# A recommender with attention over 200 history rows: items gathered whole, shorter user steps, and part of the head's second layer on GpSimd

## The chip, the cores and the metric

The kernel runs on one core of a Trainium2 chip, in float32. The metric is the device time of one execution in microseconds. Several executions are timed and their median is given; one further execution is recorded by the hardware profiler, and all views of the profile (chain of waits, costliest groups, timeline, windows) are of that one. The engines are named as in the profile: PE is TensorE, PEld its weight loads, DVE is VectorE, ACT is ScalarE, POOL is GpSimd, SP is SyncE, which only issues DMAs. ACTq and SPq are DMAs issued on these engines' queues.

## The reference

There are 16384 samples, each with a user id, an item id, a category id and a history of 200 item ids. User and item tables have 100000 rows of 64 floats, the category table has 1000.

```python
u, it, c = u_emb[user], i_emb[item], c_emb[cate]
h = i_emb[hist]                                  # 200 x 16384 x 64
feat = concat([h, itb, h - itb, h * itb], -1)    # itb: it for every history row
a = dice(feat @ au_W1 + au_b1, au_alpha, axis=1) # 36 units, moments over the samples
w = a @ au_W2 + au_b2
cur = sum(w * h, axis=0)
z = concat([u, it, c, cur], -1)                  # 256 features
z = dice(z @ W1 + b1, alpha1, axis=0)            # 80 -> here 64 and 16 units
z = dice(z @ W2 + b2, alpha2, axis=0)
out = z @ W3 + b3

def dice(x, alpha, axis):
    p = sigmoid((x - mean(x, axis)) * rsqrt(var(x, axis) + 1e-8))
    return x * (p + alpha * (1 - p))
```

## The kernel before

The samples are cut into 8 column tiles of 2048 (`ND = 8`, index `c`). A column tile is `TD = 16` gathers of 128 rows: one gather is one indirect DMA on GpSimd (line 125), which writes 128 rows of 64 floats into one of 16 places of a buffer `rows`. There are five `rows` buffers. VectorE transposes a full buffer into a tile of features by samples (four instructions of line 153), 128 partitions by 1024 columns: two groups of 64 features, each with half of the samples. Line 158 is the helper `layer`, which does almost all matmuls, in halves of 512 columns.

**Side tiles.** For six of the eight column tiles, `SIDES = (1, 3, 4, 5, 6, 7)`, the sixteenth set of 128 rows is not gathered. Its rows are asked for one by one, with 256-byte DMAs whose addresses are read from `addrs`, some on SP's queue and some on ScalarE's (line 323, helper `ask`); column tile 5 does so in one history row of three. When all 128 have landed, VectorE passes a fence (line 344) and copies them into `rows` (line 387). GpSimd so issues fewer gathers.

**Prologue.** The items' rows are fetched and transposed to `itT[0..7]`, one column tile after the other (`fetch_all`, `ask_all`, then `place_tile` and `transpose`, lines 538 to 554). Between them the category embeddings are built by matmul: for each of 16 halves `q` VectorE makes eight one-hot tiles (line 501, ring of eight `xs`), TensorE multiplies them by the category table in two groups of 64 columns (line 505), ScalarE copies the sum out (line 509) and sends it to DRAM (line 516). `attention_weights` runs at the first column tile, `head_weights` (63 DMAs on SP and some VectorE work) after the last. Both order the engines' work by hand: under `tc.manual_schedule` each engine runs its instructions in the order written.

**History.** 200 history rows by 8 column tiles are 1600 steps `k`; 180 rows run in a hardware loop of two passes, 20 are written out. `step(k)` fetches rows for `k`, transposes and multiplies for `k - 1`, evacuates and measures `k - 2`, and weighs and adds into `curT` for `k - 9`, once the moments of that history row are known.

**User steps.** At the end ten steps `j` fetch the user rows, finish the last history steps, and do the first layer of the head for `c = j - 1`: `px` gets the 64 + 64 units of `w1a`, `ph[:32]` the other 16 + 16 of `w1b`. The products of category, item and `curT` come first, then those of the user rows (line 671). ScalarE evacuates `px` (line 623) and `ph` (line 631, 32 partitions by 512 columns, twice), VectorE takes batch statistics (line 581). In each step ScalarE also computes a gate (line 361) of a history step still to be weighed, VectorE the product `y` (line 364), and TensorE `wb` of both.

**Rest of the head.** After the moments (lines 590 to 613), the second layer runs over `c`: `dice` does a sigmoid on ScalarE (line 684), an affine on ScalarE (line 686) for odd `c` or else on VectorE (line 688), and a product on VectorE (line 689); then the matmuls of `w2a`, and those of `w2b` (line 705) for four column tiles at a time, in 32-row quarters. Then come moments again, the third layer, transposes, the bias and the output's DMAs.

Of the kernel before, what the change touches and what calls it, by code (L numbers as in the profile page):

```python
# [36 lines left out]
def din_kernel(  # L37
# [76 lines left out]
    ids = [make(f"ids{i}", P, NC, dt=I32) for i in range(2)]  # L114
    side = [make(f"side{i}", P, D) for i in range(3)]
# [117 lines left out]
    w2b = make("w2b", P, P)  # L233
    w3 = make("w3", P, 4, P)
    b1a = make("b1a", P, 1)
    b1b = make("b1b", S, 1)
# [9 lines left out]
    def head_weights():  # L246
        for t in (w1a, w1b, w2a, w2b, w3, bias2, al2):
            nc.vector.memset(t, 0.0)
        w1 = W1.rearrange("(f d) z -> d f z", d=D)
        for e in range(2):  # L250
            for g in range(2):
                r, d = quarter(e, g), ts(e, S)
                for f in (slice(0, 2), slice(3, 4)):
                    nc.sync.dma_start(w1a[r, f, ts(g, ZA)], w1[d, f, :ZA])
                    nc.sync.dma_start(w1b[r, f, ts(g, ZB)], w1[d, f, ZA:])
        for g in range(2):

            nc.sync.dma_start(w1a[ts(g, D), 2, ts(g, ZA)], w1[:, 2, :ZA])
            nc.sync.dma_start(w1b[ts(g, D), 2, ts(g, ZB)], w1[:, 2, ZA:])
            nc.sync.dma_start(w2a[ts(g, ZA), g * ZA : g * ZA + Z2], W2[:ZA])  # L260
            nc.sync.dma_start(b1a[ts(g, ZA)], col(b1)[:ZA])
            nc.sync.dma_start(ala[ts(g, ZA)], col(alpha1)[:ZA])
            nc.sync.dma_start(b1b[ts(g, ZB)], col(b1)[ZA:])
            nc.sync.dma_start(bias2[g * ZA : g * ZA + Z2], col(b2))
            nc.sync.dma_start(al2[g * ZA : g * ZA + Z2], col(alpha2))
            for j in range(4):
                r = slice(j * S + g * ZB, j * S + (g + 1) * ZB)
                nc.sync.dma_start(w2b[r, g * ZA : g * ZA + Z2], W2[ZA:])
                w = j * S + g * ZO
                nc.sync.dma_start(w3[g * ZA : g * ZA + Z2, j, w : w + ZO], W3)  # L270
                nc.sync.dma_start(alb[r], col(alpha1)[ZA:])
        nc.sync.dma_start(bias3, b3.partition_broadcast(P))
        for t, u in ((ala, al1a), (alb, al1b), (al2, al12)):
            nc.vector.tensor_scalar(u, t, -1.0, 1.0, ALU.mult, ALU.add)

        for t, n in ((same_a, ZA), (same_b, ZB)):
            nc.vector.tensor_single_scalar(lane, lanes, n - 1, ALU.bitwise_and)
            nc.vector.tensor_copy(t, lane)
            nc.vector.tensor_scalar(t, t, 0.0, n / P, ALU.is_equal, ALU.mult)
# [57 lines left out]
    def ask_all(s, split, first, n, at, table):  # L337
        for queue, runs in enumerate(shares(NS * P // ND, s, split)):
            runs = [(r0, min(end, n * P)) for r0, end in runs if r0 < n * P]
            ask(queue, runs, first, range(n), at, table)  # L340

# [47 lines left out]
    def fetch_all(k, c, ids, table):  # L389
        for n in range(TD - (c in SIDES)):  # L390
            j = column(c, n)
            gather(rows[k % ROWS], ids[:, j : j + 1], n, table)
# [91 lines left out]
    def order_categories():  # L484
        for c in range(ND):
            n, j = TD - (c in SIDES), column(c, 0)
            nc.scalar.dma_start(cs[c][:, :n], columns(r_cate)[:, j : j + n])
            if c in SIDES:
                j = column(c, TD - 1)
                nc.scalar.dma_start(cs[c][:, n:], col(r_cate[j * P : (j + 1) * P]))  # L490
        nc.scalar.dma_start(table, c_emb.rearrange("(b p) d -> p b d", p=PB))
# [26 lines left out]
    with tc.manual_schedule():  # L518
        nc.sync.dma_start(ids[0], columns(r_item))
        load_addresses(2, r_item.rearrange("(o b) -> o b", o=1))  # L520
        nc.vector.memset(hm, 0.0)
        nc.scalar.copy(hT[SPREAD], hm)
        order_categories()
        load_hist_ids(0, 0)
        load_addresses(0, r_hist[0:1])
        nc.sync.dma_start(ids[1], columns(r_user))
        nc.gpsimd.iota(lanes, pattern=[[1, P]], base=P, channel_multiplier=-1)
        for q in range(SPREAD - 1):
            spread_categories(q)
# [4 lines left out]
        scale_addresses(2)  # L534
# [3 lines left out]
        for c in range(ND + 1):  # L538
            if c < ND:
                fetch_all(c, c, ids[0], i_emb)  # L540
                ask_all(c, 0.56, -NS, NS, addr[2], i_emb)
                for q in (2 * c, 2 * c + 1):
                    pick_categories(q)
                    if q + SPREAD - 1 < HALVES:
                        spread_categories(q + SPREAD - 1)
                    if q:
                        store_categories(q - 1)
            if c == 0:
                attention_weights()
                scale_addresses(0)  # L550
            if c:
                if c - 1 in SIDES:
                    place_tile(c - 1, SIDES.index(c - 1) - NS)
                transpose(itT[c - 1], rows[(c - 1) % ROWS])
# [12 lines left out]
        head_weights()  # L567
# [10 lines left out]
    zst = [make(f"zst{i}", P, n, STATS) for i, n in enumerate((2 * ND, 4, 2 * ND))]  # L578

    def measure_head(i, j, t, h):  # L580
        nc.vector.bn_stats(zst[i][:, 2 * j + h, :], t[:, ts(h, CH)])

# [34 lines left out]
    def head_layer(pairs):  # L617
        layer(px, [(w1a[:, f], t) for f, t in pairs], last=False)
        layer(ph[:S], [(w1b[:, f], t) for f, t in pairs], last=False)
# [6 lines left out]
    def head_units(c):  # L626
        evacuate(za[c], px, b1a, 0, c)
        if c == ND - 1:
            start_moments("z", 0, 2, 0, same_a)
        for h in range(2):  # L630
            nc.scalar.activation(
                zb[c // 4][ts(c % 4, S), ts(h, CH)], ph[:S, ts(h, CH)], AF.Identity, bias=b1b
            )
            if c % 4 == 3:
                measure_head(1, c // 4, zb[c // 4], h)

    with tc.manual_schedule():
        steps(BODY, L - BODY, L - BODY, r_user.rearrange("(o b) -> o b", o=1))
        U = addr[(L - BODY) % 3]
        j = column(SIDES[-1], TD - 1)  # L640
        nc.sync.dma_start(sidx[0], col(r_user[j * P : (j + 1) * P]))
        first = -(-tiles_by_address(L - BODY)[0] // 3) * 3

        weighed = {*range(-LAG, K - LAG), K, K + 1}
        for j in range(ND + 2):
            if j < ND:
                fetch_all(K + j, j, ids[1], u_emb)
                if j == SIDES[-1]:
                    gather(rows[(K + j) % ROWS], sidx[0], TD - 1, u_emb)
                nc.sync.dma_start(category[j % 2], catT[j])  # L650
            step(K + j, K - 1, weighed)
            weighed.add(K + j - LAG)
            left = [k for k in range(K) if k not in weighed]
# [5 lines left out]
            if j < ND:  # L659
                ask_all(j, SPLIT, first, NS - 1, U, u_emb)  # L660
            if 1 <= j <= ND:
                c = j - 1
                head_layer(((2, category[c % 2]), (1, itT[c]), (3, curT[c])))
                if c in SIDES[:-1]:
                    place_tile(K + c, first + SIDES.index(c))
                parts = (0, TD) if c < ND - 1 else (0, TD - 4, TD)
                for n in map(slice, parts, parts[1:]):
                    transpose(user[c % 2], rows[(K + c) % ROWS], n)
                    for dst, w in ((px, w1a[:, 0]), (ph[:S], w1b[:, 0])):
                        for i in range(2):  # L670
                            nc.tensor.matmul(
                                by_tile(dst, i)[:, n], w, by_tile(user[c % 2], i)[:, n],
                                start=False, stop=n.stop == TD, skip_group_check=True,
                            )
                head_units(c)
# [4 lines left out]
        def dice(dst, z, norm, al1, al, parts=1, scalar=False):  # L680
            p = temps[next(turns) % len(temps)]
            for i in range(parts):
# [4 lines left out]
                else:  # L687
                    nc.vector.tensor_scalar(p[:, c], p[:, c], al1, al, ALU.mult, ALU.add)
                nc.vector.tensor_mul(dst[:, c], p[:, c], z[:, c])
# [5 lines left out]
        ab = ucT[:2]  # L695

        beside = {0: range(4), 4: range(4, 6), 6: range(6, 8)}
        for c in range(ND + 2):
            if c < ND:
                if c % 4 == 0:  # L700
                    dice(ab[c // 4], zb[c // 4], nb, al1b, alb, 2 if c == 0 else 1, c > 0)
                for i in range(2):
                    for k in beside.get(c, ()):
                        r = ts(k % 4, S)
                        nc.tensor.matmul(
                            pz[k % 4][:, ts(i, CH)], w2b[r], ab[k // 4][r, ts(i, CH)],
                            start=True, stop=False, skip_group_check=True,
                        )
                dice(curT[c], za[c], na, al1a, ala, 2 if c == 0 else 1, c % 2 == 1)
                layer(pz[c % 4], [(w2a, curT[c])], first=False)  # L710
# [70 lines left out]
```

## Time and profile before

| | |
|---|---|
| time, median of 3 runs | 31195.79 us (31191.82 to 31199.41) |
| profiled execution, its own time | 31199.79 us |
| its span in the profile | 31198.0 us |
| mean granted TensorE clock | 0.809 |
| PE, PEld busy | 20922.2 us (67%), 8551.5 us (27%) |
| DVE busy | 15705.3 us (50%) |
| ACT busy | 3823.8 us (12%) |
| POOL busy | 23418.8 us (75%), 24783 instructions |
| DMA | 907.51 MB, mean 29 GB/s |

Busy time does not count the issue of a DMA by its engine, so an engine that issues one DMA after the other shows as busy for only part of the time. In the groups, a line gives engine, operation, output and inputs, the count, busy time and mean duration, and at the end how long the engine had been idle just before these instructions, with what ended most of that. In the timeline a line gives start, duration, engine, line, operation, and in brackets the idle time before it and what released it; instructions of one kind that follow each other closely are put into one line with their count.

### The profile page before, as it was taken

The page shows a single profiled execution, that of the slowest core. Times are in us where ns is not written, and L with a number is a line of the kernel's source. Part 1 is how long each engine was busy: PE and PEld are TensorE (multiplying, and loading weights), DVE is VectorE, ACT ScalarE, POOL GpSimd, SP SyncE. Part 2 cuts the span into 40 slices and gives each one's busy share as a digit, 9 for nine tenths or more (in the row PEclk, how much of TensorE's full clock was granted, in tenths as well). Part 3 has the DMA queues.
Part 4 walks back from the last instruction along what each step waited for, and adds up shares of the span by engine and source line. Part 5 has one row for each costly group of instructions (what it writes and reads, how often), then busy time and mean ns, then how long its engine had stood idle before and what let it go on. Part 6 is the DMA issues. An engine that isn't in the chain of part 4 may idle for free.

```text
span 31198.0 us, 427397 instructions
## 1 busy us (share of the span) xinstructions
PE 20922.2 (67%) x39376; PEld 8551.5 (27%) x39376; DVE 15705.3 (50%) x21745; ACT 3823.8 (12%) x3330; POOL 23418.8 (75%) x24783
## 2 busy tenths in 40 slices
PE   5666666666666666666666666666666666666667
PEld 2222222222222222222222222222222222222222
DVE  4555554554555555555455455555555555545554
ACT  1111111111111111111111111111111111111111
POOL 6777777777777777777777777777777777777776
PEclk7888888888888888888888888887888888888888
DMA  2111111111111111111111111111111111111111
GB/s 41 29 29 29 29 29 29 29 29 29 29 29 29 29 29 29 29 29 29 29 29 29 29 29 29 29 29 29 29 29 29 29 29 29 29 29 29 29 29 30
DMA packets 1135469, 907.51 MB, mean 29 GB/s; under 512 B 730704, under 2 KB 730704, under 8 KB 1132426
## 3 DMA queue, kind: packets, MB, share of 16 engines
q0 software_dynamic: 792896, 813.51, 13.9%
q1 hardware_dynamic: 193404, 35.89, 0.8%
q10 hardware_dynamic: 146125, 30.64, 0.7%
q14 instruction: 2734, 22.39, 0.2%
q8 instruction: 310, 5.08, 0.1%
HBM read 873.55 MB, written 4.39 MB: 28 GB/s over the span
## 4 chain that ended last, share of the span: by engine, by line
POOL 32%; issue 12%; PE 5%; DMA 4%; DVE 2%; ACTq 1%; ACT 0%; DVEq 0%; POOLq 0%
POOL rows L125 32%; DMA rows<-in_L_rec_i_emb,idx 4%; PE px L158 2%; PE ph L158 1%; PE wb L158 1%; ACTq L323 1%; DVE hT L153 1%; DVE wb L368 0%; DVE curT L369 0%; ACT pg L361 0%; DVE st L377 0%; ACTq L315 0%; ACT xs L372 0%; DVE y L364 0%; DVE hm L400 0%
## 5 line engine op out<-in xcount | busy, mean ns | idle before, releaser
L125 POOL DMA_INDIRECT rows<-in_L_rec_i_emb,idx x24400 | 23038.6, 944 | 7542.4 <-issue 7198.7
L158 PE MATMUL ph<-hT,unit 128*128 128x512 f32 x6404 | 5928.7, 1077 | 9820.7 <-DVE hT L153 9820.2
L368 DVE SCALAR_TENSOR_TENSOR wb<-wb,au_bias,hT 128x1024 f32<-128x1024 f32 x1609 | 2080.3, 1293 | 9802.6 <-PE wb L158 9802.6
L158 PEld LDWEIGHTS ph<-hT,unit 128*128 128x128 f32 x6404 | 1747.3, 305 | 12865.9 <-DVE hT L153 12687.8
L153 DVE STREAM_TRANSPOSE hT<-rows 64x512 f32<-64x512 f32 x6404 | 4517.0, 705 | 1483.9 <-DMA rows<-in_L_rec_i_emb,idx 894.5
L158 PE MATMUL px<-hT,blk_h 128*128 128x512 f32 x6404 | 4125.0, 733 | 0.0
L372 ACT ACTIVATE xs<-px,au_bias 128x1024 f32<-128x1024 f32 x1602 | 1783.6, 1113 | 14375.2 <-PE wb L158 10720.9
L158 PE MATMUL wb<-y,blk_p 128*128 128x512 f32 x6436 | 3318.4, 597 | 246.6 <-DVE y L364 246.1
L361 ACT ACTIVATE pg<-xs,sh,rs 128x1024 f32<-128x1024 f32 x1609 | 1943.0, 1208 | 12481.6 <-issue 9985.6
L158 PE MATMUL px<-itT,blk_i 128*128 128x512 f32 x6404 | 3355.8, 606 | 0.0
L158 PE MATMUL wb<-xs,blk_x 128*128 128x512 f32 x6436 | 3300.5, 594 | 5.3 <-DVE curT L369 5.3
L158 PE MATMUL px<-hm,blk_m 128*128 128x512 f32 x6408 | 3011.2, 592 | 0.0
L400 DVE TENSOR_TENSOR hm<-ph,itT 128x1024 f32<-128x1024 f32 x1601 | 1960.6, 1225 | 1920.1 <-PE ph L158 1920.0
L364 DVE TENSOR_TENSOR y<-pg,xs 128x1024 f32<-128x1024 f32 x1609 | 1959.4, 1218 | 1293.7 <-ACT pg L361 1291.5
L158 PEld LDWEIGHTS px<-hT,blk_h 128*128 128x128 f32 x6404 | 1649.9, 258 | 2417.9 <-issue 2363.7
L377 DVE BATCH_NORM_STATS2 st<-xs 128x6 f32<-128x512 f32 x3204 | 2058.9, 685 | 60.8 <-ACT xs L372 17.1
L369 DVE TENSOR_TENSOR curT<-wb,curT 128x1024 f32<-128x1024 f32 x1609 | 1970.4, 1225 | 54.8
L158 PEld LDWEIGHTS px<-itT,blk_i 128*128 128x128 f32 x6404 | 1402.0, 219 | 2031.2 <-issue 2031.2
L158 PEld LDWEIGHTS wb<-y,blk_p 128*128 128x128 f32 x6436 | 1215.2, 191 | 1847.9 <-issue 1460.7
L158 PEld LDWEIGHTS wb<-xs,blk_x 128*128 128x128 f32 x6436 | 1224.6, 190 | 1551.9 <-issue 1544.4
L158 PEld LDWEIGHTS px<-hm,blk_m 128*128 128x128 f32 x6408 | 1217.4, 190 | 1532.9 <-issue 1520.3
L387 DVE COPY rows<-side 128x64 f32<-128x64 f32 x1079 | 235.7, 218 | 485.0 <-DMA side<-in_L_rec_i_emb 472.9
(184 smaller groups left out, 2044.3 us busy)
## 6 DMA issues: line engine op xcount, KB each, us to landing
side<-in_L_rec_i_emb SPq DMA_DIRECT2D x68720, 0.2 KB
side<-in_L_rec_i_emb ACTq DMA_DIRECT2D x68624, 0.2 KB
rows<-in_L_rec_i_emb,idx POOLq DMA_INDIRECT x24400
idx<-in_r_hist SPq DMA_DIRECT2D x200, 61.0 KB
hT<-cs ACTq DMA_DIRECT2D x16, 500.0 KB
side<-in_L_rec_u_emb SPq DMA_DIRECT2D x336, 0.2 KB
side<-in_L_rec_u_emb ACTq DMA_DIRECT2D x304, 0.2 KB
ucT<-catT SPq DMA_DIRECT2D x8, 512.0 KB
```

Of the source, the lines that this page charges most:

```text
L125: nc.gpsimd.indirect_dma_start(out=dst[:, n, :], out_offset=None, in_=table, in_offset=bass.IndirectOffsetOnAxis(ap=ids, axis=0),)
L153: nc.vector.transpose(by_tile(dst[ts(e, D)], i)[:, n], of[ts(i, D), n, ts(e, S)])
L158: nc.tensor.matmul(dst[:, ts(i, CH)], lhsT, rhs[:, ts(i, CH)], start=(first and j == 0), stop=(last and j == len(pairs) - 1), skip_group_c ...
L323: dma = issue.dma_start(side[m % 3].bitcast(U8)[p : p + 1], flat[ds(a, ROW)].rearrange("(o d) -> o d", o=1),).then_inc(landed[m % 3], 16)
L361: nc.scalar.activation(pg, xs[k % XR], AF.Sigmoid, bias=shifts[i], scale=rstds[i])
L364: nc.vector.tensor_mul(y, pg, xs[k % XR])
L368: nc.vector.scalar_tensor_tensor(wb, wb, au_bias2, hT[k % LAG], ALU.add, ALU.mult)
L369: nc.vector.tensor_add(curT[k % ND], wb, curT[k % ND])
L372: nc.scalar.activation(xs[k % XR], px, AF.Identity, bias=au_bias)
L377: nc.vector.bn_stats(stats[l % 3][:, 2 * c + i, :], xs[k % XR][:, ts(i, CH)])
L387: nc.vector.tensor_copy(rows[k % ROWS][:, TD - 1], side[m % 3])
L400: nc.vector.tensor_mul(hm, ph, itT[k % ND])
```

## The change

- **Items.** All 128 item gathers are done on GpSimd, with the ids of the six side tiles loaded into `side_ids` by six small DMAs. `ask_all`, the items' addresses, fences and copies are gone from the prologue.
- **Order of the prologue.** The category ids are loaded in turn with their spreading, the history's first ids and addresses at `c == 0`; the user ids and `head_weights` come at `c == 2`.
- **User steps.** 126 tiles are gathered, and two (column tiles 3 and 5) are asked for row by row, on SP's queue alone, 48 rows a step. The products of category and item stand before the gate and weights of the step, those of `curT` after. `ph` is now 128 partitions by 256 columns: four quarters of 32 output partitions, each by a matmul of at most 256 columns, evacuated by one instruction and measured by one. There are nine steps.
- **Second layer.** `w2b` is laid out as two matrices with zero rows, used 64 rows at a time right after `w2a` of the same `c`. Affine and product of `curT[3]`, `ab[1]` and `curT[6]` are done on GpSimd; two of these affines were on ScalarE, the third on VectorE.

The diff, without the parts that only declare or reload:

```diff
+    def load_all_ids(i, v):
+        for s in range(NS):
+            j = NC + s
+            nc.sync.dma_start(side_ids[i][:, s : s + 1], col(v[j * P : (j + 1) * P]))
+
-    def fetch_all(k, c, ids, table):
-        for n in range(TD - (c in SIDES)):
+    def fetch_all(k, c, i, table, by_address=()):
+        for n in range(TD):
             j = column(c, n)
-            gather(rows[k % ROWS], ids[:, j : j + 1], n, table)
+            at = ids[i][:, j : j + 1] if j < NC else side_ids[i][:, j - NC : j - NC + 1]
+            if j - NC not in by_address:
+                gather(rows[k % ROWS], at, n, table)
...
         for c in range(ND + 1):
             if c < ND:
-                fetch_all(c, c, ids[0], i_emb)
-                ask_all(c, 0.56, -NS, NS, addr[2], i_emb)
+                fetch_all(c, c, 0, i_emb)
                 for q in (2 * c, 2 * c + 1):
                     pick_categories(q)
...
             if c == 0:
                 attention_weights()
+                load_hist_ids(0, 0)
+                load_addresses(0, r_hist[0:1])
                 scale_addresses(0)
+            if c == 2:
+                nc.sync.dma_start(ids[1], columns(r_user))
+                load_all_ids(1, r_user)
+                head_weights()
             if c:
-                if c - 1 in SIDES:
-                    place_tile(c - 1, SIDES.index(c - 1) - NS)
                 transpose(itT[c - 1], rows[(c - 1) % ROWS])
...
-        head_weights()
...
-    def head_layer(pairs):
-        layer(px, [(w1a[:, f], t) for f, t in pairs], last=False)
-        layer(ph[:S], [(w1b[:, f], t) for f, t in pairs], last=False)
+    def head_layer(pairs, first=False, last=False, n=(0, TD)):
...
+        for j, (f, t) in enumerate(pairs):
+            for r in range(4):
+                n0 = r % 2 * TD // 2
+                of = slice(max(n[0], n0), min(n[1], n0 + TD // 2))
+                if of.start < of.stop:
+                    to = slice(of.start - n0, of.stop - n0)
+                    nc.tensor.matmul(
+                        ph[ts(r, S), :QH].rearrange("p (n t) -> p n t", t=S)[:, to],
+                        w1b[:, f], by_tile(t, r // 2)[:, of],
+                        start=first and j == 0, stop=last, skip_group_check=True,
+                    )
...
-        for h in range(2):
-            nc.scalar.activation(
-                zb[c // 4][ts(c % 4, S), ts(h, CH)], ph[:S, ts(h, CH)], AF.Identity, bias=b1b
-            )
-            if c % 4 == 3:
-                measure_head(1, c // 4, zb[c // 4], h)
+        nc.scalar.activation(others(c), ph[:, :QH], AF.Identity, bias=b1b)
+        nc.vector.bn_stats(zst[1][:, c, :], others(c))
...
+        tiles = [SIDES.index(c) for c in (3, 5)]
...
-        for j in range(ND + 2):
+        for j in range(ND + 1):
+            c = j - 1
             if j < ND:
-                fetch_all(K + j, j, ids[1], u_emb)
-                if j == SIDES[-1]:
-                    gather(rows[(K + j) % ROWS], sidx[0], TD - 1, u_emb)
+                fetch_all(K + j, j, 1, u_emb, tiles)
                 nc.sync.dma_start(category[j % 2], catT[j])
             step(K + j, K - 1, weighed)
             weighed.add(K + j - LAG)
+            runs = [(r0, r0 + LOAD) for r0 in (2 * LOAD * j, 2 * LOAD * j + LOAD)]
+            runs = [(r0, min(end, len(tiles) * P)) for r0, end in runs if r0 < len(tiles) * P]
+            ask(0, runs, first, tiles, U, u_emb)
+            if j:
+                head_layer(((2, category[c % 2]), (1, itT[c])), first=True)
             left = [k for k in range(K) if k not in weighed]
             if j >= 2 and left:
                 gate(left[0])
                 weights(left[0])
                 weigh(left[0])
                 weighed.add(left[0])
-            if j < ND:
-                ask_all(j, SPLIT, first, NS - 1, U, u_emb)
...
+            if j:
+                head_layer(((3, curT[c]),))
...
         for c in range(ND + 2):
+
+            if c == 0:
+                dice(ab[0], zb[0], nb, al1b, alb, 2)
+            if c < ND and c not in (3, 6):
+                dice(curT[c], za[c], na, al1a, ala, 2 if c == 0 else 1, c % 2 == 1)
+            if c in (0, 3):
+                dice(curT[c + 3], za[c + 3], na, al1a, ala, engine=nc.gpsimd)
+            if c == 1:
+                dice(ab[1], zb[1], nb, al1b, alb, engine=nc.gpsimd)
             if c < ND:
-                if c % 4 == 0:
-                    dice(ab[c // 4], zb[c // 4], nb, al1b, alb, 2 if c == 0 else 1, c > 0)
...
-                layer(pz[c % 4], [(w2a, curT[c])], first=False)
+                layer(pz[c % 4], [(w2a, curT[c])], last=False)
+                for r in (0, 2, 1, 3):
+                    of = ts(r // 2, D)
+                    nc.tensor.matmul(
+                        pz[c % 4][:, ts(r, QH)], w2b[of, r % 2], ab[c // 4][of, ts(c % 4, QH)],
+                        start=False, stop=r % 2 == 1, skip_group_check=True,
+                    )
```

`dice` takes the engine of its affine and product as an argument.

## The prediction

> **What bounds the kernel now.** I read the page's chain first, then its costliest group.
>
> ```profile
> POOL 32%; issue 12%; PE 5%; DMA 4%; DVE 2%; ACTq 1%; ACT 0%; DVEq 0%; POOLq 0%
> ...
> L125 POOL DMA_INDIRECT rows<-in_L_rec_i_emb,idx x24400 | 23038.6, 944 | 7542.4 <-issue 7198.7
> ```
>
> The chain is POOL's gathers: 0.944 us of work and some 0.30 us of issue, from start to start 1.2485 us in the timeline. 24778 gathers (the engine's 24783 instructions less five) at that pitch are 30935 us of a span of 31198.0, and from 299.65 us to the first user gather at 30925.42 us POOL almost never rests (mean pitch 1.2499). The change leaves the order of instructions in all history steps as it is, so the time can move only before 300 us, after 30925 us, and by the number of gathers. So I asked for POOL's timeline at the start.
>
> ```profile
> 177.08 0.94 POOL L125 DMA_INDIRECT rows<-in_L_rec_i_emb,ids  x1 [0.31 <-issue]
> 245.98 0.94 POOL L125 DMA_INDIRECT rows<-in_L_rec_i_emb,idx  x1 [67.96 <-DVE itT L153]
> ...
> 280.71 0.94 POOL L125 DMA_INDIRECT rows<-in_L_rec_i_emb,idx  x1 [14.82 <-DVE itT L153]
> ```
>
> The 122 item gathers and the first five of the history are done at 178 us; then POOL waits for a free rows buffer, that is, for VectorE to transpose an item tile. Beyond the usual 0.30 us the two waits are 67.65 and 14.52 us: 82.2 us. Why VectorE is late, the timeline of all engines tells:
>
> ```profile
> 97.95 19.47 ACTq L323 DMA_DIRECT2D side<-in_L_rec_i_emb  x42
> ...
> 117.52 0.58 ACT L509 COPY y<-pg 128x512 f32<-128x512 f32 x1 [25.38 <-issue]
> ...
> 118.15 2.83 PE L505 MATMUL pg<-xs,curT 125*64 125x512 f32 x6 [19.79 <-ACT y L509]
> ```
>
> A copy on ScalarE stands behind 42 row requests, TensorE waits 19.79 us for the copy, VectorE for TensorE; each of eight item tiles takes about 35 us where its 16 gathers need 20. The third thing is the port:
>
> ```profile
> 53.49 11.31 POOL L125 DMA_INDIRECT rows<-in_L_rec_i_emb,ids  x1 [0.30 <-issue]
> ...
> 54.01 10.67 DVE L501 TENSOR_SCALAR xs<-hT,values 125x1024 f32<-125x1024 int32 x16
> ```
>
> One gather lasts as long as sixteen one-hots running back to back (0.667 us each): 10.36 us lost. Where TensorE paces the one-hots at 0.858 us, gathers last 1.41 us (+0.47). All loss of this sort is 23.6 us: the 32nd history gather starts at 299.65 us, the first gather at 2.88 us; 153 pitches make 191.0 of the 296.8 us between them, the two waits 82.2, and 23.6 are left (the 122 item gathers' mean of 1133 instead of 944 ns makes 23.1).
>
> **The end.** From the first user gather to the last evacuation of head layer 1 it takes 198.1 us, while the gathers end at 31078.7 us: here TensorE decides.
>
> ```profile
> 30925.40:31123.50 198.10, 164.34 (x349) 55.35 (x350) 77.81 (x113) 27.67 (x37) 116.05 (x123) 0.93 0.17 41
> 31123.50:31132.50 9.00, 2.33 (x12) 1.80 (x12) 5.87 (x22) 2.66 (x5) 0.00 (x0) 0.77 0.00 0
> 31132.50:31162.20 29.70, 22.98 (x64) 8.27 (x64) 25.02 (x33) 26.98 (x33) 0.00 (x0) 0.90 0.00 0
> ```
>
> Columns: span, then busy time of PE, PEld, DVE, ACT, POOL. A user step takes 20.7 us: ScalarE evacuates and gates (the gate waits behind the evacuations), TensorE waits 2.63 us for the product, then 2.84 us wb, 5.15 px, 5.27 ph, and 1.91 + 1.85 for the user part. The third row is the second layer: ScalarE 26.98 of 29.7 us.
>
> **Items gathered whole.** Six gathers more: +7.5 us of POOL. Gone are the 768 row requests (430 on SP's queue, 338 on ScalarE's), the six fences and copies. ScalarE's copies then follow TensorE at once; a tile costs VectorE 16 one-hots (10.7 us) and one transpose (2.9), TensorE 13.7 us warm, both under POOL's 20. VectorE's waits for attention weights (about 19 us) and for the head weights, now at the third tile (25.3 us for their 63 DMAs on SP in the trace, which stand ahead of nothing urgent), are covered by five rows buffers: gather 81 needs the first transpose at about 113 us, and that comes near 63; gather 97 the second at about 137, and that comes near 105. Without that cover each such us would be POOL's. So all 82.2 us go. What comes next is the port. Per tile about 11 one-hots run free before TensorE paces the last five (ring of eight, 0.858 against 0.667 us). Bounds: yielding as at 22.6–28 us (gathers 1.02 instead of 0.94: 0.5 us a tile) plus 1.2 for the paced part is 1.7 us a tile, 13.6 in all; held as at 53.49 is 7.0 + 1.2 = 8.2 a tile, 65.6 in all, and 83 if all 16 run free. The trace has one free run of each sort, so I take half and half: 40. Prologue: 82.2 − 7.5 − (40 − 23.6) = **58.3 us** (ends 15.3 and 84.7).
>
> The Trainium skill (SBUF — State Buffer, "Who interferes with whom") says that whoever issues first holds the pair VectorE and GpSimd share "for the whole instruction". Read so, a gather waits for one one-hot at most, and some 49 gathers beside the one-hots would lose at most 32 us, 8 less than I take; the row of 11.31 us shows sixteen in a row, so I stay with the rows.
>
> **Head weights earlier.** The loads hid behind the loop but for VectorE's 13.45 and 4.93 us after it, which reached POOL as 2.7 us at 28511: **2.7 us** (0 to 2.7).
>
> **User steps.** 126 gathers for 123: +3.7 us POOL, inside the next number. ScalarE asks for no rows (17.5 us of queue per step gone); SP asks for two tiles, 48 rows a step, and the second is whole near +101 us, needed at +120. The ph passes become four of 32 output columns by 256, side by side. The trace has the like: in L505 two 64-column products start 2 ns apart and run together. If four do, ph costs 1.3 + 0.5 instead of 5.27 + 1.85, and a step 15 us of TensorE; the first two steps end at about +43 and +70 instead of +48 and +78.7, six more at 15 give +160. The last gather starts at 125 × 1.2485 = 156.1, lands 4.2 us later; transpose and products of its four columns make 162. So POOL decides, just: 198.1 − 162 = **36.1 us**. If no two overlap, a step costs about 20 and 15 us are left; nothing in these rows makes it a loss.
>
> **Moments and second layer.** One statistic of 256 columns in place of two of 512 at the end: 0.7 us (0 to 1). Of ScalarE's 26.98 us two Identities (1.24 each) go; of VectorE's 25.02 three products (1.22) and one affine (0.81). The w2b products (each pass 0.43 us, 32 of them, px to wb together) are spread over the tiles. POOL is idle here (0.00), and its order is fixed: third tile, ab's second half, sixth. A pair costs 2.03 us on VectorE, the lower end; no row has it on POOL. By the order above they are due about 12, 16 and 20 us into the stage, starting near 5: up to 5 us a pair is hidden. The upper end I take from the slowest POOL row, 11.31 us for each of six instructions: 68 − 15 = 53 us late. VectorE's rows are nearer, as the tiles and operations are the same: gain **1.5 us** (2.5 to −53).
>
> The skill (GPSIMD Engine Reference, "When to use GPSIMD" and the sections before it) speaks against this part: elementwise work about twice as slow as VectorE, 4497 ns at 2048 elements, and about 6 us for a first call. Twice the rows is some 4 us a pair by that page, an estimate: still hidden, with the first call about level.
>
> **Sum.** 58.3 + 2.7 + 36.1 + 0.7 + 1.5 = 99.3 us. On the profiled execution (31199.8, its span 31198.0 and 1.8 around it) that is 31100.5; it lies 4.0 above the median, 31195.8, from which it is **31096.5**.
>
> **Rivals.** (a) VectorE holds the port through every free run: 65.6 to 83 instead of 40, 31122 to 31139. For it: the 11.31 us row. Against: eight one-hots at 22.6–28 us let gathers through. 0.16. (b) It yields in all: 13.6 instead of 40, 31070. 0.14. (c) The column groups run one after the other: 21 us less gain, 31118. For it: the old 32-column passes took a full 0.43 us; against: L505's pairs. 0.07. (d) The change doesn't free POOL: tiles still take VectorE and TensorE 35 us each and the waits stay; only the tail's 41 us come, 31155. Against: the ScalarE queue was the last wait. 0.07. (e) Slower: GpSimd's three pairs in sequence become the bound of the second layer. They are hidden up to 15 us in all, so they cost 3p − 15; the rest gains 98, so it decides from p = 38 us a pair; at p = 45 it is 31218. For it: no POOL arithmetic in the trace, a POOL instruction that took twelve times its usual while VectorE was busy; against: VectorE does a pair in 2.03. 0.05.
>
> **How the numbers follow.** The forecast, 31082 to 31112, has 0.51. About 0.2% (62 us, below 31133) is what a measurement can tell from no change. Faster: 0.51 + 0.14 + 0.07 and 0.13 of (a): 0.85. Same: the rest of (a) and (d), 0.10. Slower 0.05. The range goes from (b), less a few us, to (a)'s upper end: 31065 to 31141; above it are (d) and (e).
>
> **What would show it.** POOL's gathers without a wait for itT from start to the user rows, the 32nd history gather near 241 us instead of 299.65; gathers of 5 to 11 us counted in the item stage; no row requests on ScalarE before the loop; ph rows in fours that start together; the user phase 162 us with POOL its releaser; POOL pairs of 2 to 5 us in the second layer. A wait of POOL for itT over 10 us, or VectorE waiting for POOL's product, would prove the working wrong.

## The result and the profile after

The changed kernel takes 31083.38 us (median of 6 runs, 31081.74 to 31085.82); the kernel before took 31196.67 us in the same comparison (31191.82 to 31202.58). The ratio is 0.9963 (95% interval 0.9952 to 0.9974), 113 us less. The forecast was 31096.5, with 31065 to 31141 as the range. The profiled execution took 31084.14 us, its span is 31082.4 us, 115.6 us under that of before. Six of the runs below fell on two other chips ("the slow chip" of their expectations), where every kernel took over 50000 us, the one before 51232 and 50820; of these six only what stands at the start or in the second layer is used.

The page's chain and first group are what they were, and so is the pitch of the gathers:

```profile
POOL 32%; issue 12%; PE 5%; DMA 4%; DVE 2%; ACTq 0%; ACT 0%; DVEq 0%; POOLq 0%
...
L126 POOL DMA_INDIRECT rows<-in_L_rec_i_emb,idx x24400 | 23036.9, 944 | 7456.8 <-issue 7185.5
```

The idle time ahead of the history's gathers (third number) fell from 7542.4 to 7456.8 us. POOL's timeline at the end of the items shows why: the last item gather and the first of the history follow each other without a wait.

```profile
184.10 0.94 POOL L126 DMA_INDIRECT rows<-in_L_rec_i_emb,ids  x1 [0.30 <-issue]
185.35 0.94 POOL L126 DMA_INDIRECT rows<-in_L_rec_i_emb,side_ids  x1 [0.30 <-issue]
186.59 0.94 POOL L126 DMA_INDIRECT rows<-in_L_rec_i_emb,idx  x1 [0.30 <-issue]
187.84 0.94 POOL L126 DMA_INDIRECT rows<-in_L_rec_i_emb,idx  x1 [0.30 <-issue]
```

The whole difference, by marks that both traces have (in us; negative is faster):

| stretch | before | after | difference | forecast |
|---|---|---|---|---|
| start to the 32nd history gather | 299.65 | 225.28 | −74.4 | −58.3 |
| from there to the first user gather | 30625.8 | 30621.1 | −4.7 | −2.7 |
| to the first sigmoid of the second layer | 206.9 | 169.2 | −37.8 | −36.8 |
| second layer, to its last evacuation | 30.4 | 33.0 | +2.6 | −1.5 |
| rest | 35.2 | 33.8 | −1.4 | 0 |
| sum | | | −115.6 | −99.3 |

The rest is code that wasn't changed; in the runs below it lies between 33.7 and 35.0, so most of −1.4 can be scatter. The history stretch lies between 30618.3 and 30622.8 in six runs below that share the changed prologue, so some 2 of its 4.7 us can be scatter too.

Two places of the new trace were not as predicted. The first is the item stage, POOL and then VectorE:

```profile
44.56 0.94 POOL L126 DMA_INDIRECT rows<-in_L_rec_i_emb,ids  x1 [0.30 <-issue]
45.81 11.72 POOL L126 DMA_INDIRECT rows<-in_L_rec_i_emb,ids  x1 [0.30 <-issue]
57.83 0.95 POOL L126 DMA_INDIRECT rows<-in_L_rec_i_emb,ids  x1 [0.30 <-issue]
...
45.55 0.55 DVE L146 TENSOR_SCALAR addrs<-addrs 1x768 int32<-1x768 int32 x1 [2.23 <-DMA addrs<-in_r_hist]
46.03 10.67 DVE L502 TENSOR_SCALAR xs<-hT,values 125x1024 f32<-125x1024 int32 x16
```

Again one gather, and only one, was held through sixteen one-hots (11.72 us instead of 0.94). In the other seven tiles the gathers got through, at 1.02 us beside one-hots that run freely and 1.41 us beside those that TensorE paces; such a tile lost 1.0 to 2.2 us. The second place is the second layer, in windows that begin and end with the stage (columns: span, then busy time of PE, PEld, DVE, ACT, POOL, the granted clock last but two). After, and the same window of before:

```profile
31015.54:31048.58 33.04, 26.17 (x96) 11.52 (x96) 27.02 (x30) 25.57 (x31) 14.13 (x6) 0.86 0.00 1
```

```profile
31132.35:31162.79 30.44, 22.98 (x64) 8.27 (x64) 25.56 (x34) 27.72 (x33) 0.00 (x0) 0.90 0.00 0
```

ScalarE lost 2.15 us of work as intended, but the stage is longer: TensorE has 3.2 us more, and VectorE, which lost three products and an affine, has 1.5 us more. VectorE's and POOL's timelines show the latter:

```profile
31019.71 1.68 POOL L703 TENSOR_SCALAR ucT<-ucT,al1a,ala 128x1024 f32<-128x1024 f32 x1 [16.33 <-ACT ucT L699]
31021.47 2.67 POOL L704 TENSOR_TENSOR curT<-ucT,hT 128x1024 f32<-128x1024 f32 x1
31024.13 2.72 POOL L703 TENSOR_SCALAR y<-y,al1b,alb 128x1024 f32<-128x1024 f32 x1
31026.94 3.21 POOL L704 TENSOR_TENSOR ucT<-y,xs 128x1024 f32<-128x1024 f32 x1
31030.14 1.19 POOL L703 TENSOR_SCALAR ucT<-ucT,al1a,ala 128x1024 f32<-128x1024 f32 x1
31031.41 2.67 POOL L704 TENSOR_TENSOR curT<-ucT,hT 128x1024 f32<-128x1024 f32 x1
...
31022.04 3.19 DVE L704 TENSOR_TENSOR curT<-ucT,hT 128x1024 f32<-128x1024 f32 x1
...
31031.91 3.26 DVE L704 TENSOR_TENSOR curT<-ucT,hT 128x1024 f32<-128x1024 f32 x1
```

A product of VectorE takes 3.19 and 3.26 us beside POOL's, 1.20 to 1.23 alone. A pair of affine and product on POOL (two lines each above) took 4.35, 5.93 and 3.86 us.

### The profile page after: what moved, and what is told of

Same layout as the page of the kernel before. It is cut to its first block, busy times and chain, and to the rows that moved or that the text cites. A ratio compares the mean times of both kernels' runs of the same rounds, so it can differ in the third digit from the quotient of the medians.

```text
span 31082.4 us, 425363 instructions
## 1 busy us (share of the span) xinstructions
PE 20879.6 (67%) x39536; PEld 8540.5 (27%) x39536; DVE 15702.9 (51%) x21735; ACT 3814.6 (12%) x3320; POOL 23440.5 (75%) x24798
## 3 DMA queue, kind: packets, MB, share of 16 engines
q0 software_dynamic: 793184, 813.81, 11.9%
## 4 chain that ended last, share of the span: by engine, by line
POOL 32%; issue 12%; PE 5%; DMA 4%; DVE 2%; ACTq 0%; ACT 0%; DVEq 0%; POOLq 0%
POOL rows L126 32%; DMA rows<-in_L_rec_i_emb,idx 4%; PE px L159 2%; PE ph L159 1%; PE wb L159 1%; DVE hT L154 1%; DVE wb L364 0%; ACTq L324 0%; DMA rows<-in_L_rec_i_emb,sidx 0%; DVE curT L365 0%; PE px L629 0%; DVE st L373 0%; DVE hm L403 0%; DVE ucT L154 0%; DVE rows L383 0%
## 5 line engine op out<-in xcount | busy, mean ns | idle before, releaser
L126 POOL DMA_INDIRECT rows<-in_L_rec_i_emb,idx x24400 | 23036.9, 944 | 7456.8 <-issue 7185.5
```

What stands on the lines that cost most here:

```text
L126: nc.gpsimd.indirect_dma_start(out=dst[:, n, :], out_offset=None, in_=table, in_offset=bass.IndirectOffsetOnAxis(ap=ids, axis=0),)
```

## The experiments

The chips differ a little: the kernel before took 31196.7 us where the changed kernel was timed, 31202.3 and 31201.0 in the two comparisons below. Differences under some 6 us are therefore read from marks in the traces, not from medians of different comparisons.

**The prologue alone.** The kernel before, with the prologue of the changed one; user steps and second layer as before, except that the users' rows go through the new `fetch_all`:

```diff
-                fetch_all(K + j, j, ids[1], u_emb)
-                if j == SIDES[-1]:
-                    gather(rows[(K + j) % ROWS], sidx[0], TD - 1, u_emb)
+                fetch_all(K + j, j, 1, u_emb, range(NS - 1))
```

> The kernel before, with the prologue of the changed one alone (items gathered whole, its order, head weights at the third tile); user steps and second layer as before. Theory: the 32nd history gather starts near 225 us as in the changed kernel, and the user phase takes 198 us as before: 76 to 81 us faster than before. Rival: part of what came at the start needs the other parts (less than 70), or all of it was the start (over 100).

Measured: 31127.19 us (31115.71 to 31129.56), 75.1 under the kernel before on that chip, ratio 0.9976 (0.9966 to 0.9985). The 32nd history gather starts at 223.70 us, as it should, and the first user gather at 30846.51, 78.9 us earlier than before. So the prologue is worth some 79 us by itself, head weights included; its parts (row requests, fences and copies, order of loads) were not tried apart. That the median shows 75 only comes from the end: from first user gather to last evacuation the profiled run took 208.6 us, against 200.7 in the kernel before with the same instructions. The windows show a granted clock of 0.92 against 0.99 in the last 120 us or so. It is why single-stage gains of a few us are not read from the total here.

**The held gather.** The int32 affine of the history's addresses (line 146) moved from ahead of the second tile's one-hots to behind the third's:

```diff
                 load_addresses(0, r_hist[0:1])
-                scale_addresses(0)
             if c == 2:
                 nc.sync.dma_start(ids[1], columns(r_user))
                 load_all_ids(1, r_user)
+                scale_addresses(0)
                 head_weights()
```

> The changed kernel, but the int32 affine of the history's first addresses is done by VectorE behind the one-hots of the third item tile, not right ahead of those of the second. Theory: the one gather of 11.72 us comes from that instruction being busy when the gather starts, which puts the gather's first access into a run of one-hots without a gap; moved away, the second tile's run lets gathers through like the other seven (1 to 2.2 us lost instead of 10.8): 8.5 to 10 us faster than the changed kernel. Rival: the run after VectorE's long wait holds the port whatever stands before it: within 1.5 us.

Measured: 31073.03 us (31070.96 to 31075.34), ratio 0.9959 (0.9946 to 0.9973). POOL's timeline, and VectorE's run below it:

```profile
40.39 0.98 POOL L126 DMA_INDIRECT rows<-in_L_rec_i_emb,ids  x1 [0.30 <-issue]
41.68 1.08 POOL L126 DMA_INDIRECT rows<-in_L_rec_i_emb,ids  x1 [0.31 <-issue]
43.06 1.02 POOL L126 DMA_INDIRECT rows<-in_L_rec_i_emb,side_ids  x1 [0.30 <-issue]
...
41.19 10.70 DVE L502 TENSOR_SCALAR xs<-hT,values 125x1024 f32<-125x1024 int32 x16
```

The 32nd history gather starts at 214.15 us instead of 225.28, and all that POOL loses before it falls from 23.9 to 12.7 us. The theory held: no gather is held, and the gain, 11.1 us up to this mark, is a little over the 8.5 to 10 expected.

**Shifted runs.** Is it the instruction, or only where a gather starts in a one-hot?

```diff
                 fetch_all(c, c, 0, i_emb)
+                if c >= 3:
+                    nc.vector.bn_stats(stats[0][:, 0, :], hm[:, :460])
```

> The changed kernel, with one more VectorE instruction (statistics of 460 zeros, result unused, about 0.6 us) ahead of the one-hots of each of item tiles 3 to 7. Theory: what decides is where in a one-hot a gather starts: more than 0.5 us in, it gets through (1.02 us); about 0.25 us in, it waits for the first gap of the run. The instruction shifts the first, so that a gather starts about 0.25 us into a one-hot; each of the five runs then holds one gather for 7 to 11 us, and the time grows by 25 to 45 us. Rival: a held gather needs the int32 instruction, or a run that starts after a long wait: no gather over 2 us in these five tiles, time within 4 us of the changed kernel.

Measured: 31080.69 us (31079.26 to 31081.68), ratio 0.9961 (0.9948 to 0.9975); no gather over 2 us in tiles 3 to 7. The theory of this run failed, its rival came true. In tiles 5 and 7 a gather does start about 0.25 us into a one-hot, which was to be the bad phase, and it gets through in 1.28 and 1.30 us. Tile 5, POOL and VectorE:

```profile
140.23 1.28 POOL L126 DMA_INDIRECT rows<-in_L_rec_i_emb,ids  x1 [0.30 <-issue]
...
139.40 0.64 DVE L543 BATCH_NORM_STATS2 st<-hm 128x6 f32<-128x460 f32 x1
139.95 11.29 DVE L502 TENSOR_SCALAR xs<-hT,values 125x1024 f32<-125x1024 int32 x16
```

In the second tile, where the affine still stands, the gather was held as before (11.83 us).

**The affine ahead of the runs.** On top of the moved affine:

```diff
                 fetch_all(c, c, 0, i_emb)
+                for _ in range(max(0, c - 2)):
+                    nc.vector.tensor_scalar_mul(addr[0], addr[0], 1)
```

> The kernel that has the int32 affine moved behind the third tile's one-hots (31073.0 us), with such an instruction (times one, on the same row of 768) put right ahead of the one-hots of item tiles 3 to 7: one of them for tile 3, two for tile 4, up to five for tile 7. Theory: a gather that starts while that instruction is busy, with one-hots right behind it, is held until the run has a gap; where several stand in a row some gather must start in them, so at least tiles 5 to 7 hold a gather for 7 to 11 us, and the time is 20 to 50 us longer. Rival: the one long gather was a coincidence of phase, not of the instruction: no gather over 3 us, the time longer by the affines alone, under 5 us.

Measured: 51095.98 us (51011.82 to 51131.73, before 51232.14), too scattered to tell tens of us. The trace answers it all the same: each of the tiles 3 to 7 holds one gather, of 10.47, 10.98, 11.49, 11.49 and 11.38 us. The last of them, and VectorE beside it:

```profile
247.17 0.98 POOL L126 DMA_INDIRECT rows<-in_L_rec_i_emb,side_ids  x1 [0.30 <-issue]
248.46 11.38 POOL L126 DMA_INDIRECT rows<-in_L_rec_i_emb,ids  x1 [0.30 <-issue]
260.14 0.95 POOL L126 DMA_INDIRECT rows<-in_L_rec_i_emb,ids  x1 [0.30 <-issue]
...
246.20 2.91 DVE L543 TENSOR_SCALAR addrs<-addrs 1x768 int32<-1x768 int32 x5
249.04 10.67 DVE L502 TENSOR_SCALAR xs<-hT,values 125x1024 f32<-125x1024 int32 x16
```

The gather starts while the affine is busy, and one-hots follow without a gap. The kernel with w2b first (below), without the added affines, ran on the same chip and has no gather over 1.6 us there. Five of five: the affine between a gather under way and a run of one-hots is enough.

The other traces settle more. In all 14, eleven runs of one-hots had this affine directly ahead of them and a gather under way beside it; all eleven held the gather, for 10.47 to 11.89 us. In four more the affine stood there while POOL had no gather under way, and none was held. No other gather in the first 320 us of any trace took over 1.54 us. The place of the gather is not the cause: the held ones began from 0.96 us ahead of the first one-hot to the same instant, and gathers that began in that stretch behind other instructions got through. The nearest case is the second tile of the kernel with w2b first (run again, below), where another affine of VectorE, and not the int32 one, stands ahead of the same sixteen one-hots; POOL, then VectorE:

```profile
43.91 1.30 POOL L126 DMA_INDIRECT rows<-in_L_rec_i_emb,ids  x1 [0.30 <-issue]
...
44.20 0.23 DVE L228 TENSOR_SCALAR unit<-unit 128x128 f32<-128x128 f32 x1
44.34 10.70 DVE L502 TENSOR_SCALAR xs<-hT,values 125x1024 f32<-125x1024 int32 x16
```

What it is in the int32 affine that does this stays open.

**The pairs back on ScalarE and VectorE.**

```diff
-                dice(curT[c + 3], za[c + 3], na, al1a, ala, engine=nc.gpsimd)
+                dice(curT[c + 3], za[c + 3], na, al1a, ala, scalar=c == 0)
             if c == 1:
-                dice(ab[1], zb[1], nb, al1b, alb, engine=nc.gpsimd)
+                dice(ab[1], zb[1], nb, al1b, alb, scalar=True)
```

> The changed kernel, but the three pairs of affine and product of the second layer are back on ScalarE (affines of curT[3] and ab[1]) and VectorE (the rest). Theory: the pairs on GpSimd cost time, because VectorE's products lasted up to 3.19 and 3.26 us instead of 1.22 beside them; the second layer's stage (first sigmoid to last evacuation, 33.0 us in the changed kernel, 30.4 before) falls to 29 to 31 us, and the time by about 2 to 4 us against the changed kernel. Rival: the pairs help, as predicted (1.5 us), and the stage grew by the finer w2b products; then the stage is 34 to 36 us and the time 1 to 3 us longer.

Measured: 31082.95 us (31081.58 to 31084.14), ratio 0.9962 (0.9949 to 0.9976). Its window of the second layer:

```profile
31012.94:31046.09 33.15, 26.34 (x96) 11.82 (x96) 25.56 (x34) 27.83 (x33) 0.00 (x0) 0.86 0.00 1
```

33.15 us with the pairs off POOL, 33.04 with them on it. Neither the theory nor the rival: moving the pairs changes nothing here. What stays the same in both windows is TensorE: 96 matmuls, 26 us. As this run has no work on POOL in the stage and still takes 2.7 us more than before, GpSimd is not needed for the loss; what is left is the w2b part of the edit, and the order of the pairs, which this run keeps and which was not tried apart.

**w2b first.** With the affine moved as above:

```diff
-                layer(pz[c % 4], [(w2a, curT[c])], last=False)
                 for r in (0, 2, 1, 3):
...
-                        start=False, stop=r % 2 == 1, skip_group_check=True,
+                        start=r % 2 == 0, stop=False, skip_group_check=True,
                     )
+                layer(pz[c % 4], [(w2a, curT[c])], first=False)
```

> The changed kernel with the int32 affine behind the third tile's one-hots (as in the run that moved only that, 31073.0 us), and in the second layer w2b's products ahead of w2a's. Theory: TensorE decides the second layer now, and it starts 4.6 us into the stage, when curT[0] is there, with slow first products; w2b can start with ab[0], about 3.3 us in: the stage falls from 33.0 to 31.5 to 32 us, and the time to about 31072. Rival: ScalarE or the pairs on GpSimd decide: the stage stays at 33.0, the time at 31073.

Measured: 51085.60 us (51035.41 to 51116.35, before 51232.14). The second layer took 31.91 us, against 33.04, 33.03 and 33.29 in three kernels with w2b behind on that chip. And again:

> The kernel with w2b's products ahead of w2a's and the int32 affine moved, again, since the first time fell on a chip where all kernels, the one before too, took over 51000 us. There the second layer's stage was 31.9 us as expected (33.0 in the others). Theory: TensorE's start decides, 31.5 to 32 us, and the whole lies 9 to 13 us under the changed kernel (31083). Rival: the stage gained is lost in the third layer, 31073 or more.

Measured: 31070.96 us (31069.82 to 31073.72), ratio 0.9958 (0.9944 to 0.9972), the fastest of all. The stage is 31.91 us. TensorE's first products in the stage, in the changed kernel and in this one:

```profile
31020.17 3.88 PE L159 MATMUL px<-curT,w2a 128*128 128x512 f32 x4 [7.29 <-DVE curT L704]
31023.98 1.48 PE L726 MATMUL px<-ucT,w2b 64*128 64x256 f32 x8
```

```profile
31004.85 2.08 PE L724 MATMUL px<-ucT,w2b 64*128 64x256 f32 x8 [4.92 <-ACT hm L699]
31007.13 3.02 PE L159 MATMUL px<-curT,w2a 128*128 128x512 f32 x4 [0.20 <-DVE curT L704]
```

TensorE starts 2.3 us into the stage (which begins at 31002.59) instead of 4.6 (there 31015.54), and some of its slow first products lie in time that was idle. Against the run that only moved the affine, the stage gained 1.1 us and what follows it took 0.9 us more (34.7 against 33.7, within its scatter), so the total is the same within what can be told.

**w2b left out.**

```diff
-                layer(pz[c % 4], [(w2a, curT[c])], last=False)
-                for r in (0, 2, 1, 3):
...
+                layer(pz[c % 4], [(w2a, curT[c])])
```

> The changed kernel with the products of w2b in the second layer left out (the result so lacks 16 of the 80 features there). Theory: TensorE decides the second layer in the changed kernel, 2.98 us a tile of which w2b has 1.1; without it ScalarE decides, 25.6 us of work, and the stage falls from 33.0 to 26.5 to 29 us, the time by 4 to 6.5. Rival: ScalarE's and VectorE's chain decides with or without w2b, as it did before (30.4): then the stage is 31 to 33 us.

Measured: 50657.24 us (50607.72 to 50682.65, before 50820.42). The stage took 31.72 us, against 33.03 on the same chip in the run with the head weights late (the last one below), whose second layer is that of the changed kernel: the rival's. TensorE now waits for VectorE, as its lines show (the bracket is the wait), and VectorE for its shared products:

```profile
50549.28 3.47 PE L159 MATMUL ph<-curT,w2a 128*128 128x512 f32 x4 [1.22 <-DVE curT L704]
50559.47 3.48 PE L159 MATMUL px<-curT,w2a 128*128 128x512 f32 x4 [3.28 <-DVE curT L704]
...
50556.06 3.26 DVE L704 TENSOR_TENSOR curT<-ucT,hT 128x1024 f32<-128x1024 f32 x1
```

So the 33.0 us have two holders that lie close together: TensorE with w2b, and behind it VectorE's products stretched by POOL. Taking away either alone gives 1.3 us or nothing. Both together were not tried.

**ph in a row.** In the user steps, the four quarters of `ph` in the same 32 output partitions:

```diff
-                        ph[ts(r, S), :QH].rearrange("p (n t) -> p n t", t=S)[:, to],
+                        ph[:S, ts(r, QH)].rearrange("p (n t) -> p n t", t=S)[:, to],
...
-        nc.scalar.activation(others(c), ph[:, :QH], AF.Identity, bias=b1b)
+        for r in range(4):
+            nc.scalar.activation(
+                others(c)[ts(r, S)], ph[:S, ts(r, QH)], AF.Identity, bias=b1b[:S]
+            )
```

> The changed kernel, but the four quarters of ph are made in the same 32 output partitions, one beside the other in columns, so that the four products of a set can't run side by side (and ScalarE evacuates them in four pieces). All else in the user steps is as in the changed kernel. Theory: a ph set of four then takes about 1.85 us instead of 0.46; four sets a step make a step 5 to 6 us longer, and the user phase (162.7 us) becomes 195 to 210 us. Rival: the gathers decide the user phase, or the row requests taken from ScalarE were the gain; then it stays below 172 us.

Measured: 51103.71 us (51042.41 to 51122.19, before 51232.14). Its user phase is not used, and that version lacked a part of the sums of `ph`, as two quarters that share a bank both began theirs with a start. With one start a bank, once more:

> The changed kernel with the four quarters of ph in the same 32 output partitions, beside each other in columns, so that they can't run side by side; the first time it fell on the slow chip, and the start of the sums was not right there. Theory: a set of four takes about 1.85 us instead of 0.46, a step 5 to 6 us more, and the user phase 195 to 210 us instead of 162.7. Rival: the gathers decide, or the freed ScalarE queue was the gain: it stays below 172 us.

Measured: 31108.93 us (31106.46 to 31111.72), ratio 0.997 (0.9959 to 0.9982). The user phase took 189.8 us against 162.7. The same products in the changed kernel and here:

```profile
30966.51 0.64 PE L639 MATMUL ph<-ucT,w1b 128*32 128x256 f32 x8
30966.97 0.61 PE L639 MATMUL ph<-itT,w1b 128*32 128x256 f32 x8
```

```profile
30963.72 1.91 PE L639 MATMUL ph<-ucT,w1b 128*32 128x256 f32 x8
30965.47 1.89 PE L639 MATMUL ph<-itT,w1b 128*32 128x256 f32 x8
```

A set takes 0.46 us from start to start side by side, 1.75 in a row; 27.1 of the 37.8 us hang on that. The time missed the expected 195 by 5 us: the steps in the middle took 19.2 to 19.7 us, against 16.2 to 17.5 in the changed kernel, some 2 us more and not 5 to 6; only the first two and the last grew by 4.6 to 5.1. In the last 110 us the granted clock was 1.00 here, and 0.92 in the last 83 us of the changed kernel, and TensorE's waits shrank (0.41 to 0.89 us for VectorE's transpose instead of 1.69 to 1.97). The rival fell clearly.

**Head weights late.** `head_weights()` behind the last item tile again:

> The changed kernel, but the head weights are loaded after the last item tile again, as before. Theory: their 63 DMAs then come behind the loop and stop VectorE there, which reaches POOL as a wait of 2 to 3 us some 600 us later; the start is not changed by more than 2 us, as POOL had no wait there; 2 to 5 us slower than the changed kernel. Rival: the 27 us that VectorE waited for these DMAs at the third item tile cost something at the start after all; then this kernel is faster.

> The changed kernel with the head weights' 63 DMAs behind the last item tile, as before; the first time it fell on the slow chip. Theory: VectorE's waits for them come behind the loop again and reach POOL as one wait of 2 to 4 us; the start (32nd history gather at 225 us) stays within 2 us; 2 to 5 us slower than the changed kernel. Rival: VectorE's 27 us of waiting at the third item tile cost the start something: then the start is earlier than 222 us and the time not longer.

Measured: 51056.47 us (50987.38 to 51137.83, before 51232.14) and 50603.13 us (50589.81 to 50674.79, before 50820.42). The changed kernel itself was not timed on these chips, so this term is not settled. What can be said is from the other runs: all on the first chips that have the head weights in the prologue lack the 2.72 us wait of POOL at 28511 us, and POOL has no wait for an item's transpose although VectorE waited 27.1 us for these DMAs.

## Why the prediction was right, and where its steps were off

**The prologue.** POOL was freed as predicted: with the new prologue it never waits for `itT`; both waits, 82.2 us, went, for 7.5 us of gathers, and VectorE's 27.1 us stop cost POOL nothing. That the row requests on ScalarE's queue were the cause is read from the trace of before (a copy behind 42 of them); no run took them away alone. A slip in the reading of that trace changes no sum: all gathers up to 178 us carry `ids`, so they are the 122 of the items, and the first one of the history is that at 245.98. The mis-sized term is the port: 40 us taken, 23.9 measured up to the 32nd history gather. The two sorts of run were sized well (1.0 to 2.2 us a yielding tile, 1.7 predicted; 10.8 for the held one, 8.2 to 10.4), but half and half was wrong. A gather is held in one run of sixteen one-hots in each of the two traces, and both runs follow the int32 affine. The trace of before showed it, busy while the held gather (53.49) started, and it was not read:

```profile
53.48 0.60 DVE L145 TENSOR_SCALAR addrs<-addrs 1x768 int32<-1x768 int32 x1
54.01 10.67 DVE L501 TENSOR_SCALAR xs<-hT,values 125x1024 f32<-125x1024 int32 x16
```

The port's term accounts for the 16 us by which the prologue beat the forecast. The rule of the Trainium skill (SBUF — State Buffer, "Who interferes with whom"), that whoever issues first holds the shared pair for one whole instruction, fits the 1.02 and 1.41 us, and not the gathers of 10.5 to 11.9, which waited through 15 or 16 instructions.

**User steps.** The sum came out, in part by luck. By the mark that the working used (its 198.1 us end where the last evacuation starts) the phase took 161.1 us, predicted 162; by the end of that evacuation, the mark used here, it went from 200.7 to 162.7. But the first two steps gained 12.6 us where 8.7 were worked out, and the other six 24.4 where 27.4 were, and the two errors offset each other: a step in the middle took TensorE's chain 17.2 us, not 15, with waits for VectorE's transposes and ScalarE's evacuations that the working left out; and the last step's products ran without a wait for a gather. So TensorE, not POOL as predicted, still decides the phase, and the two are level. That the column groups run side by side is shown by the run that put them in a row. It leaves 10.7 of the 37.8 us to the rest of the edit, of which the parts were not tried apart.

**Second layer.** Here a step failed: "The w2b products (each pass 0.43 us, 32 of them, px to wb together) are spread over the tiles" was costed at nothing. In the trace of before four and later two 32-row products ran at once, 7.8 us of TensorE's time in all, and the first of them, slow ones (1.06 to 1.21 us each, 0.59 to 0.69 later), lay where it had nothing else to do, as its lines of before show:

```profile
31134.61 1.19 PE L705 MATMUL px<-ucT,w2b 32*128 32x512 f32 x1 [4.92 <-ACT hm L684]
31134.62 1.21 PE L705 MATMUL ph<-ucT,w2b 32*128 32x512 f32 x1
...
31138.34 2.08 PE L158 MATMUL px<-curT,w2a 128*128 128x512 f32 x4
```

Now they come in pairs, 1.1 us a tile and 9.4 in all, and TensorE begins when `curT[0]` is there, not with `ab[0]`, and its slow first products are those of `w2a` (3.88 us for four, 1.98 later). The pairs on POOL, 3.9 to 5.9 us, were inside the 5 us of slack but for one; what the working left out is that they slow VectorE's products from 1.2 to 3.3 us. VectorE never waited for POOL's product, the sign that would have proved this part of the working wrong. The stage lost 2.6 us where 1.5 were to be gained. The rival in which GpSimd becomes the bound was far off. The estimate for a pair by the Trainium skill (GPSIMD Engine Reference, "When to use GPSIMD" and the sections before it), about 4 us, fits two of the three measured (4.35 and 3.86 us, not 5.93), and its 6 us for a first call did not show: the first affine on POOL began 0.1 us after its input was ready, 16.3 us after POOL's configuration instructions.

## What to carry to other kernels

When a shared resource costs either little or much, look for what stands ahead of each of the two in the trace before taking the middle: here the small int32 instruction in front of a run of one-hots was worth 10 to 11 us. A copy that a pipeline needs should not stand behind dozens of row requests on the same queue: in the trace of before POOL lost 82 us behind such a queue, by the reading above. Moving work to an idle engine gains nothing where the stage is then held by another; the start of the stage (TensorE waiting 4.6 us for its first operand, 2.3 with `w2b` first) was worth 1.1 us, three pairs of affine and product nothing.

## What was not expected of the hardware

A gather that is under way while a 1 x 768 int32 affine of VectorE is busy, with one-hots right behind, waits through the whole run (10.5 to 11.9 us in all eleven such runs of the traces), while a gather that starts some 0.5 us into a one-hot takes 1.02 us. A VectorE product with both inputs in SBUF takes 3.2 us instead of 1.2 beside a product on GpSimd. The same user steps took 200.7 us at a granted clock of 0.99 and 208.6 at 0.92 in their second part.

The fastest version of all is the changed kernel with the affine moved and w2b first, 31070.96 us, 130 us under the kernel before on its chip, where the changed kernel was 113 under it on its own.
